# Joining two tiled matmul steps of a chunked linear attention, under a list scheduler's due times

## The chip, the cores and the metric

The kernel runs on one core of a Trainium2 chip. The metric is the device time of one execution in microseconds (us). The median of three runs is compared; a separate execution was recorded by the hardware profiler.

## The reference, cut to what matters

The input `x` is (8, 1024, 256) in fp32: 8 sequences of 1024 rows. Four blocks follow each other, each as `x = x + block(layernorm(x))`:

```
# 1: flow ("linear") attention with 16 heads of width 16, then its own FFN (256 -> 1024 -> 256, gelu)
q = sigmoid(heads(Wq));  k = sigmoid(heads(Wk));  v = heads(Wv)
# sink_in, src_out, cons_sink, cons_src: cumulative sums over the rows of q and k, per head
vs = v * src_comp
kv = cumsum(einsum('bhld,bhlm->bhldm', k, vs), axis=2)        # causal state
x  = einsum('bhld,bhldm->bhlm', q * sink_in/normal, kv) * sink_alloc
h  = layernorm(inputs + x @ Wo + bo);   out = layernorm(h + gelu(h @ W1 + b1) @ W2 + b2)
# 2: dense FFN 256 -> 1024 -> 256 with relu
# 3: full softmax attention over 1024 rows, one head of width 256
# 4: gated FFN 256 -> 704 -> 256, activations and weights rounded block by block to FP4
```

The change lies in block 1. There the causal state is computed chunk by chunk: for a chunk of 128 rows, the output is the masked product `(q k^T) vs` inside the chunk plus `q` times the state `kv` of all chunks before it; then the chunk's own `k^T vs` is added to the state.

## The kernel before, in words

**Tiling.** Rows are handled in chunks of 128 and in groups of four chunks (512 rows). There are 16 groups, two to a sequence; `p` is the group, `i` the chunk in it (0 to 3), `c = 4p + i` the chunk's number. A group goes through block 1 and 2 in about 147 us, and the softmax and FP4 blocks of sequences that are finished run beside the later groups' linear attention and dense blocks, until about 2420 us.

**Engines.** TensorE (PE in the profile) does all products. It is used in two ways: full 128x128 products, and *tiled* ones, in which the array is cut into four tiles, 32x128 for the scores of four heads side by side, and 128x32 for products whose output is 32 wide. All is fp32: each matmul leaves two records in the profile, a transpose one.

**One chunk of linear attention** (`linear_chunk`, line 1284) has two tiled steps on PE:

- the *scores* (lines 1367 to 1385): 16 matmuls `kz` x `q` of tile size 32x128 into four PSUM banks. VectorE multiplies each bank with the causal mask `tri` into a tile `sc` of the pool `flow`;
- the *values* (lines 1406 to 1458): 8 matmuls `q` x `kv_sum` (the state so far), 16 matmuls `sc` x `v_pad`, both accumulating in one bank, and, but for a sequence's last chunk, 8 matmuls `k` x `vs` for the state. All have tile size 128x32. ScalarE copies the result to `xo`, VectorE masks the state's increment, GpSimd adds it to `kv_sum`, and a full product with `wo` follows.

Full products of the dense blocks (`half` x `w_in`, then `hidden` x `w_out`), of the softmax block (`n2T,wqk` makes `qT`; `n2T,qT` the scores; `vt,probT` the values) and of the FP4 block (`xqT` with `wgT` and `wuT`, `hqT` with `wdT`) fill the time between.

**Order.** The kernel is written as generators that yield what they need. `Plan.run` (line 375) is a list scheduler that runs while the program is built: of all parts it takes the one with the smallest key

```
key = wait, unripe, queue == "tensor", not stays, part[2]
```

`wait` comes from a model of each engine's durations in `Plan.took`; `stays` prefers a tiled step right behind a tiled step, with 0.3 us of leniency in `wait`; `part[2]` is the due time, `at`. Due times are sums of constants from the table `T`, and from `EARLY`, which gives other constants while the planned time lies under 130, 260, 400 and 2150 us and from there on. The order of issue on every engine is fixed by this.

**Transposes** (`flip`, line 734) go one of two ways. If the planner finds a product ready within `ahead` us, GpSimd copies the tile (`cut`), a transposing DMA issued by SP turns it (`spun<-cut`), and ScalarE copies it to its place. If it finds none (`plan.idle`), two PE transposes (`bank<-ident,...`) are used instead, and ScalarE copies from PSUM.

**Dense blocks.** `half` is a pair of transposed chunks; eight steps of `half` x `w_in`, bias and gelu or relu on ScalarE (`hidden`), and `w_out` make one half of a group. `behind` lets two `hidden` tiles be outstanding, and is emptied when the next `half` isn't ready.

Of the kernel before, what the change touches and what calls it, by code (L numbers as in the profile page):

```python
# [17 lines left out]
P = 128  # L18
# [7 lines left out]
HB = P // 2  # L26
SCW = P + HB
# [4 lines left out]
    span=-0.073, prods=0.129, pair=0.137, sums=0.037, weighted=0.239, sums2=0.231, chunk=0.625,  # L32
    scores=0.819, turn_k=0.829, xo=0.419, turn_h=0.635, step=0.092, dense=-0.115, norm=0.522,
    soft=3.5, soft1=0.277, soft2=0.575, soft3=0.75, fp4=2.397, fp4_over=4.836, tail=11,
    weights=0.209, shy=0.745, ripe_t=1.247, ripe_v=0.744, ripe_s=0.298, ripe_g=0.0, ripe_d=6.94,
    back=0.511, ahead=0.946, stage=3, lin=0.0, lin0=0.01, lin1=0.0, lin2=0.0, lin3=0.0,
    dense0=0.0, dense1=-0.033, norm0=0.0, norm1=0.0, weights0=-0.412, weights1=0.023, gate0=0,
    gate1=1, by_act=1,
)
LAG = 2  # L40
QB = 16
G = 4
GT = G * P
# [18 lines left out]
    "norm": (3, D, F32),  # L62
    "hidden": (LAG + 2, D, F32),
    "soft": (5, D, F32),
# [15 lines left out]
        prods=0.359, pair=0.052, weighted=0.011, sums2=0.405, scores=0.861, turn_k=0.81,  # L80
        xo=0.296, step=0.131, dense=0.051, soft=2.551, soft1=0.323, soft2=0.706, fp4_over=5.754,
        weights=0.044, ripe_t=1.058, ripe_v=0.456, ripe_s=0.249, ripe_g=0.541, ripe_d=9.276,
        lin3=0.344, dense1=-0.003, weights0=-1.017, weights1=0.043,
    )),
    (260.0, dict(
        span=-0.064, prods=0.185, sums=-0.114, chunk=0.702, scores=0.785, dense=-0.085,
# [4 lines left out]
        prods=-0.044, turn_k=0.82, turn_h=0.707, step=0.103, norm=0.746, soft=3.784, soft3=0.912,  # L91
        fp4=2.195, weights=0.078, ripe_d=7.2, ahead=0.839, lin2=-0.414,
    )),
    (2150.0, dict(
        prods=0.106, pair=0.211, sums=0.071, weighted=0.176, chunk=0.596, turn_k=0.801, xo=0.47,
        turn_h=0.706, soft3=1.013, fp4=3.733, fp4_over=6.383, weights=0.169, ripe_d=6.945,
        ahead=0.541, lin1=0.497, lin2=-0.186, lin3=-0.528, dense0=-0.017, dense1=0.151,
        norm0=-0.113, weights0=-0.286, gate1=3,
    )),
    (1000000000.0, dict(  # L100
        lin3=0.54, ripe_d=5.647, lin1=0.423, dense1=-0.052, scores=0.713, xo=0.287, chunk=0.609,
        shy=0.81, back=0.523, sums2=0.353,
    )),
]

# [18 lines left out]
class Plan:  # L124
# [203 lines left out]
    def pe(self, *tiles, **kw):  # L328
        return self.need("tensor", tiles, **kw)

    def dve(self, *tiles, **kw):
        return self.need("vector", tiles, **kw)
# [108 lines left out]
def block_stack_kernel(ctx: ExitStack, tc: tile.TileContext, a: dict, out: bass.AP):  # L441
# [20 lines left out]
    plan = Plan(tc, tc.nc)  # L462
# [5 lines left out]
    nc, pe, dve, act, dma = plan, plan.pe, plan.dve, plan.act, plan.dma  # L468
    x_dram = a["L0_attn_inputs"]
    B, L, _ = x_dram.shape  # L470
# [13 lines left out]
    def mm_bank():  # L484
        bank = ps.tile([P, 512], F32, tag="bank", name="bank")
        plan.bank(bank)
        return bank
# [25 lines left out]
    def small(shape, name, bufs=4):  # L513
        t = sm.tile(shape, F32, tag=name, name=name, bufs=bufs)
        return t
# [77 lines left out]
    later = make("q_c", "later")[:, : GT + P]  # L593
# [197 lines left out]
    def blocks(t, width):  # L791
        return t[:, :width].rearrange("p (b e) -> p b e", e=QB)

    def wide(v, rows, nb):
        return v.unsqueeze(2).to_broadcast([rows, nb, QB])

    def fp4(src, width, rows=P, factor=1.0):
# [7 lines left out]

        nb = width // QB
        src = src[:rows, :width]
        amax = small([P, INTER // QB], "x_amax", 2)[:rows, :nb]
        nc.vector.tensor_reduce(
            amax, blocks(src, width), AX.X, ALU.max, apply_absolute_value=True  # L810
        )
        sc = small([P, INTER // QB], "x_s", 4)[:rows, :nb]
        nc.vector.tensor_scalar(sc, amax, factor / 6.0, 1e-12, ALU.mult, ALU.max)
        rc = small([P, INTER // QB], "x_r", 3)[:rows, :nb]
        nc.vector.reciprocal(rc, sc)
# [118 lines left out]
    weights = set()  # L934
# [59 lines left out]
    def running(out, cur, carry, b, first, last):  # L994
# [14 lines left out]
    flows = B * NG  # L1009
    seqs = [{"past": {"chunks": 0}, "n2T": {}, "vt": {}, "normed": 0} for _ in range(B)]  # L1010
    groups = [
        {"res": {}, "hT": {}, "nT": {}, "turned": {}, "scaled": set(), "ran": set()}
        for _ in range(flows)
    ]
    count = {
# [268 lines left out]
    def linear_chunk(p, i, n0T, comp, qk):  # L1284
# [7 lines left out]
            banks=1,  # L1292
            when=lambda: count["v"] == c and c - count["attended"] < V_PADS and "v" in late,
        )
        bank = mm_bank()
        for k in range(2):
            nc.tensor.matmul(
                bank[:, :D],
                lhsT=n0T[:, k, here],
                rhs=wqkv[2][:, k, :],  # L1300
                start=k == 0,
                stop=k == 1,
# [27 lines left out]
        for e in range(2):  # L1330
            into_pad(nc.scalar.copy, e, 1 - e)

        by_act = p < T["by_act"]
        tile_kz = yield from fresh(
            "flow",
            act(
                qk[1],
                at=at + times["scores"] + times["step"] * i,
                when=lambda: (
                    c - count["scored"] < 2 if by_act  # L1340
                    else i in groups[p]["scaled"] and count["scored"] == c
                )
# [6 lines left out]
        kz = tile_kz.rearrange("p (k b e t) -> p k b e t", k=2, b=2, e=2)  # L1349
# [6 lines left out]
            )  # L1356
        kz = tile_kz.rearrange("p (k b n) -> p k b n", k=2, b=2)

        if by_act:
            yield pe(  # L1360
                tile_kz, qk[0], later, banks=4,
                when=lambda: i in groups[p]["scaled"] and count["scored"] == c,
            )
            count["scored"] += 1
        else:
            yield pe(tile_kz, qk[0], banks=4, tiled=True)
        banks = [mm_bank()[:, : 2 * SCW] for _ in range(4)]
        for bank in banks:
            if by_act:
                nc.tensor.matmul(  # L1370
                    bank, lhsT=later[:, GT:], rhs=later[:, : 2 * SCW], start=True, stop=False,
                    skip_group_check=True,
                )
        for k in range(2):
            for b in range(2):
                for r, bank in enumerate(banks):
                    rows = slice(32 * r, 32 * r + 32)
                    nc.tensor.matmul(
                        bank[:, k * SCW + b * P : k * SCW + P + b * HB],
                        lhsT=kz[rows, k, b, :],  # L1380
                        rhs=qk[0][rows, k, i * P + b * HB : (i + 1) * P],
                        start=not by_act,
                        stop=True,
                        skip_group_check=True,
                    )
        plan.drop(tile_kz)
        scores = []
        for bank in banks:
            sc = yield from fresh("flow", (act if by_act else dve)(bank), "sc")
            sc = sc[:, : 2 * SCW].rearrange("p (k n) -> p k n", k=2)  # L1390
            bank = bank.rearrange("p (k n) -> p k n", k=2)
# [8 lines left out]
        if not end:  # L1400
# [2 lines left out]
            kT = two((yield from fresh("lin", need, "k")))  # L1403
            yield from flip(qk[1][:, :, here], kT, near=p == 0)
        kv = past.get("kv")
        yield pe(
            pad,
            vs,
            *scores,
            *([] if kv is None else [kv]),  # L1410
            *([] if end else [kT]),
            banks=1,
            tiled=True,
            when=lambda: count["attended"] == c,
        )
# [5 lines left out]
        bank = both[:, :D]  # L1421
        for k in range(2):
            for r in range(4):
                if kv is not None:
                    nc.tensor.matmul(
                        bank[32 * r : 32 * r + 32, k * P : (k + 1) * P],
                        lhsT=kv[:, k, 32 * r : 32 * r + 32],
                        rhs=qk[0][:, k, here],
                        start=k == 0,
                        stop=False,  # L1430
                        skip_group_check=True,
                    )
        for k in range(2):
            for b in range(2):
                for r in range(4):
                    nc.tensor.matmul(
                        bank[32 * r : 32 * r + 32, k * P + b * HB : (k + 1) * P],
                        lhsT=pad[:, b, 4 * k + r, :],
                        rhs=scores[r][:, k, b * P : P + b * HB],
                        start=kv is None and k == 0 and b == 0,  # L1440
                        stop=k == 1 and b == 1,
                        skip_group_check=True,
                    )
        plan.drop(*scores)
        if not end:

            kvbank = both[:, D : D + 64].rearrange("p (k d) -> p k d", k=2)
            for k in range(2):
                for r in range(4):
                    nc.tensor.matmul(  # L1450
                        kvbank[32 * r : 32 * r + 32, k, :],
                        lhsT=kT[:, k, 32 * r : 32 * r + 32],
                        rhs=pair_columns(vs, 4 * k + r),
                        start=False,
                        stop=True,
                        skip_group_check=True,
                    )
            plan.drop(kT)
        plan.drop(vs)
        xo = two((yield from fresh("lin", act(bank), "xo")))  # L1460
        nc.scalar.copy(xo, two(bank))
# [24 lines left out]
        bank = mm_bank()  # L1486
        for k in range(2):
# [14 lines left out]
            when=lambda: half_fits(p, "hT", i // 2) and count["dense"] >= p - 1,  # L1502
# [16 lines left out]
    def dense():  # L1519
# [44 lines left out]
        def load_weights(names, used, loaded, first):  # L1564
# [3 lines left out]
            for p in range(flows):  # L1568
                for name in names:
                    for f in 2 * list(range(0, NF, 2)):  # L1570
                        yield dma(
                            at=p + 0.9 + due("weights", p) + (2 * n % 32 + (0 if first else LAG)) / 32,
                            when=lambda: n < bufs + used[0] // 2 and count["stage"] >= 2,
# [20 lines left out]
        for p in range(flows):  # L1594
            for b, (kind, ba, func) in enumerate((("hT", b1, AF.Gelu), ("nT", fb1, AF.Relu))):
                for half in range(2):
# [3 lines left out]
                    for f in range(NF):  # L1600
# [22 lines left out]
                        if f == NF - 1:  # L1623
                            count["halves"] -= 1
                        if len(behind) > LAG:
                            yield from second()
# [271 lines left out]
```

## Time and profile before

| | |
|---|---|
| median of 3 runs | 2450.55 us (2448.66 to 2452.24) |
| the profiled execution's own time | 2450.4 us |
| its span, first to last instruction | 2448.7 us |
| PE (matmuls) busy | 2419.4 us, 99% |
| VectorE (DVE) busy | 1914.3 us, 78% |
| ScalarE (ACT) busy | 1387.7 us, 57% |
| GpSimd (POOL) busy | 1276.9 us, 52% |
| transposing DMAs `spun<-cut` | 768 |

The page gives busy time by engine, then the span in 40 slices, the chain of work that ended last, and groups of instructions with the mean duration of one. The end of a matmul is modelled and overlaps its successor, so that starts are more exact than durations: back to back, two records of a 256-column matmul start 0.216 us apart. In the timeline, equal instructions that follow each other are one row: start, busy time, name, count of records, and in brackets the engine's idle time before the row and what ended it.

### The profile page before, as it was taken

Reading aid. Unit: us, or ns where it says so; the run is one execution under the profiler, and the core shown is the slowest. Engines: PE = TensorE matmul, PEld = TensorE weight load, DVE = VectorE, ACT = ScalarE, POOL = GpSimd, SP = SyncE. Lnnn points to the kernel's source line nnn. Section 1 sums busy time; section 2 is a strip of 40 time slices with the busy share of each in tenths; the row PEclk is TensorE's granted clock in tenths of the full one; section 3 lists DMA queues with packets and bytes.
Section 4 is the critical chain, followed back from the end, with each engine's and each line's share of the span. In section 5 each row is a group of like instructions: output and inputs, shape, how many; then the busy total and the mean of one; then the engine's idle time right before and its main releaser. Section 6 shows DMA issues by size and latency. Waiting matters only on the chain.

```text
span 2448.7 us, 47669 instructions
## 1 busy us (share of the span) xinstructions
PE 2419.4 (99%) x16473; PEld 1891.6 (77%) x16473; DVE 1914.3 (78%) x4152; ACT 1387.7 (57%) x2895; POOL 1276.9 (52%) x2258
## 2 busy tenths in 40 slices
PE   8999999999999999999999999999999999999999
PEld 6877777777877777777777777777777777887777
DVE  7778787878779787787877888688886978765887
ACT  5454556565565645656565565655556465555454
POOL 4354556565555656365563655546555474544342
PEclk9999999999999999999999999999999999999999
DMA  3355455564655555546555554556545555545332
GB/s 106 91 150 160 123 151 128 139 146 121 145 135 121 140 139 129 138 115 155 132 122 134 125 150 125 139 131 124 141 127 133 143 118 145 124 126 129 67 83 59
DMA packets 630897, 312.74 MB, mean 128 GB/s; under 512 B 434304, under 2 KB 619136, under 8 KB 630656
## 3 DMA queue, kind: packets, MB, share of 16 engines
q1 hardware_dynamic: 630656, 309.70, 51.3%
q8 instruction: 130, 2.13, 0.4%
q14 instruction: 111, 0.91, 0.1%
HBM read 188.17 MB, written 20.71 MB: 85 GB/s over the span
## 4 chain that ended last, share of the span: by engine, by line
PE 88%; DVE 6%; DMA 2%; POOL 2%; issue 1%; ACT 1%; SPq 0%; DVEq 0%; POOLq 0%; ACTq 0%
PE bank L422 88%; DMA spun<-cut 2%; DVE hid L422 1%; POOL cut L422 1%; DVE prod L422 1%; DVE ln_st L422 1%; DVE n L422 0%; POOL ln_rstd L422 0%; DVE sc L422 0%; DVE mx L422 0%; DVE res L422 0%; DVE u L422 0%; SPq L422 0%; POOL ln_shift L422 0%; DMA w_in<-in_L_attn_W_dram 0%
## 5 line engine op out<-in xcount | busy, mean ns | idle before, releaser
L422 PE MATMUL bank<-half,w_in 128*128 128x256 f32 x2048 | 529.2, 381 | 9.5 <-ACT half L422 6.4
L422 PE MATMUL bank<-w_out,hidden 128*128 128x256 f32 x2048 | 525.6, 383 | 1.5 <-DMA w_out<-in_L_attn_W_dram 1.4
L422 PEld LDWEIGHTS bank<-w_out,hidden 128*128 128x128 f32 x2048 | 377.4, 190 | 105.1 <-issue 45.7
L422 PEld LDWEIGHTS bank<-half,w_in 128*128 128x128 f32 x2048 | 384.5, 190 | 87.9 <-issue 22.4
L422 POOL TENSOR_SCALAR ln_ve<-ln_mv 128x1 f32<-128x1 f32 x384 | 107.1, 279 | 510.6 <-DVE ln_mv L422 489.4
L422 POOL TENSOR_TENSOR ln_rstd<-ln_ve,neghalf 128x1 f32<-128x1 f32 x384 | 251.3, 654 | 32.0
L422 ACT ACTIVATE hidden<-bank,c_L_ffn_b 128x256 f32<-128x256 f32 x256 | 120.8, 472 | 223.8 <-PE bank L422 222.0
L422 PE MATMUL bank<-n2T,qT 128*128 128x512 f32 x512 | 241.5, 594 | 0.0
L422 PE MATMUL bank<-vt,probT 128*128 128x256 f32 x1024 | 231.2, 379 | 0.0
L422 PEld LDWEIGHTS bank<-vt,probT 128*128 128x128 f32 x1024 | 194.2, 190 | 32.9 <-issue 6.9
L422 POOL COPY cut<-n 128x512 uint16<-128x512 uint16 x233 | 175.0, 757 | 79.8 <-DVE n L422 68.4
L422 ACT ACTIVATE hidden<-bank,c_L_attn_b 128x256 f32<-128x256 f32 x256 | 119.7, 469 | 170.8 <-PE bank L422 170.0
L422 POOL COPY cut<-prob 128x512 uint16<-128x512 uint16 x213 | 147.8, 716 | 92.0 <-ACT prob L422 50.4
L422 POOL COPY cut<-hid 128x512 uint16<-128x512 uint16 x172 | 116.4, 694 | 144.3 <-DVE rsum L422 66.3
L422 PE MATMUL bank<-wdT,hqT 128*128 128x256 f32 x768 | 175.9, 379 | 0.0
L422 PE MATMUL bank<-wgT,xqT 128*128 128x352 f32 x512 | 173.8, 462 | 0.5 <-ACT xqT L422 0.5
L422 PE MATMUL bank<-wuT,xqT 128*128 128x352 f32 x512 | 172.3, 459 | 0.0
L422 ACT COPY probT<-spun 128x512 uint16<-128x512 uint16 x250 | 159.6, 674 | 13.3 <-DMA spun<-cut 12.8
L422 PEld LDWEIGHTS bank<-wdT,hqT 128*128 128x128 f32 x768 | 145.6, 190 | 22.7 <-issue 1.9
L422 ACT ACT_TABLE_LOAD x124 | 159.1, 1283 | 4.4 <-PE bank L422 2.2
L422 PEld LDWEIGHTS bank<-n2T,qT 128*128 128x128 f32 x512 | 96.4, 190 | 69.7 <-issue 56.4
L422 PEld LDWEIGHTS bank<-wuT,xqT 128*128 128x128 f32 x512 | 97.3, 190 | 54.2
(272 smaller groups left out, 4831.1 us busy)
## 6 DMA issues: line engine op xcount, KB each, us to landing
w_in<-in_L_attn_W_dram SPq DMA_DIRECT2D x128, 256.0 KB
w_out<-in_L_attn_W_dram SPq DMA_DIRECT2D x128, 256.0 KB
w_in<-in_L_ffn_w_dram SPq DMA_DIRECT2D x128, 256.0 KB
w_out<-in_L_ffn_w_dram SPq DMA_DIRECT2D x128, 256.0 KB
spread<-packed SPq DMA_DIRECT2D x90, 256.0 KB
spun<-cut SPq DMA_TRANSPOSE x768
x<-in_L_attn_inputs_dram SPq DMA_DIRECT2D x64, 128.0 KB
xr<-in_L_attn_inputs_dram SPq DMA_DIRECT2D x64, 128.0 KB
```

The costliest lines, as they stand in the source:

```text
L422: ins = method(*args, **kw)
```

## The change

The scores of chunk `i` (`i` > 0) in groups 4 to 15 are no longer a PE step of their own. The chunk prepares `kz`, leaves its `score` function in `groups[p]["asked"]`, and waits until its banks exist. The values step of chunk `i - 1` waits until the next chunk has asked, demands five free PSUM banks instead of one and the next chunk's `kz` and `q`, and issues the 16 score matmuls directly behind its own. So 36 chunks of 64 are joined this way; groups 0 to 3 and each group's chunk 0 stay as they were.

```diff
+JOIN = 4
...
+        joined = p >= JOIN and i > 0
+        if joined:
+            asked = groups[p]["asked"][i] = SimpleNamespace(tile=tile_kz, run=None, banks=None)
+        elif by_act:
...
+        def score():
+            banks = [mm_bank()[:, : 2 * SCW] for _ in range(4)]
...
+            plan.drop(tile_kz)
+            return banks
+
+        if joined:
+            asked.run = score
+            yield dve(when=lambda: asked.banks is not None)
+            banks = asked.banks
+        else:
+            banks = score()
...
+        joins = p >= JOIN and i < G - 1
+        nexts = groups[p]["asked"]
+        if joins:
+            yield dve(when=lambda: i + 1 in nexts)
         yield pe(
             pad,
             vs,
             *scores,
             *([] if kv is None else [kv]),
             *([] if end else [kT]),
-            banks=1,
+            *([nexts[i + 1].tile, qk[0]] if joins else []),
+            banks=5 if joins else 1,
             tiled=True,
             when=lambda: count["attended"] == c,
         )
...
+        if joins:
+            nexts[i + 1].banks = nexts[i + 1].run()
```

The constants of the two last stretches of `EARLY` (planned time 400 to 2150 us, and from 2150 us on) are replaced by other ones, about half of them changed and some added, among them `norm` (0.522 to 0.652), `sums2` (0.231 to 0.365), `turn_h` (0.706 to 0.798) and `span` (-0.073 to 0.034) in the first, `scores` (0.713 to 0.599), `soft3` (0.75 to 1.132) and `fp4` in the second. Constants of single early groups (`lin1`, `dense0`, `norm0` and the like) are among them too, though those groups lie before 400 us.

More of the change, by code (lines that the diff above doesn't have):

```diff
@@ L94 @@
     (2150.0, dict(
[L95 to L98, printed above, removed]
+        span=0.034, prods=0.067, pair=0.211, sums=0.071, weighted=0.176, sums2=0.365,
+        chunk=0.596, turn_k=0.822, xo=0.47, turn_h=0.798, step=0.05, dense=-0.126, norm=0.652,
+        soft3=1.013, fp4=3.733, weights=0.169, ripe_s=0.404, ripe_d=6.945, ahead=0.541,
+        lin1=-0.157, lin2=-0.457, lin3=-0.528, dense0=-0.29, weights0=-0.071, weights1=0.189,
+        gate1=3, dense1=-0.093, norm0=0.859,
     )),
     (1000000000.0, dict(
-        lin3=0.54, ripe_d=5.647, lin1=0.423, dense1=-0.052, scores=0.713, xo=0.287, chunk=0.609,
-        shy=0.81, back=0.523, sums2=0.353,
+        lin3=0.291, ripe_d=5.647, lin1=0.423, dense1=-0.096, scores=0.599, xo=0.287, gate0=2,
+        chunk=0.609, back=0.523, sums2=0.353, span=-0.107, step=0.03, ripe_s=0.0, ripe_v=1.131,
+        pair=0.076, turn_k=0.932, lin=-0.077, weights1=-0.123, soft3=1.132, fp4=0.958,
+        dense=-0.015, prods=0.27, sums=0.215, weights=0.124,
     )),
@@ L1011, in block_stack_kernel @@
     groups = [
-        {"res": {}, "hT": {}, "nT": {}, "turned": {}, "scaled": set(), "ran": set()}
+        {"res": {}, "hT": {}, "nT": {}, "turned": {}, "scaled": set(), "ran": set(), "asked": {}}
         for _ in range(flows)
@@ L1357, in linear_chunk @@
         kz = tile_kz.rearrange("p (k b n) -> p k b n", k=2, b=2)
-        if by_act:
+        joined = p >= JOIN and i > 0
+        if joined:
+            asked = groups[p]["asked"][i] = SimpleNamespace(tile=tile_kz, run=None, banks=None)
+        elif by_act:
             yield pe(
@@ L1366, in linear_chunk @@
             yield pe(tile_kz, qk[0], banks=4, tiled=True)
[L1367 to L1377, printed above, removed]
-                    nc.tensor.matmul(
[L1379 to L1383, printed above, removed]
+        def score():
+            banks = [mm_bank()[:, : 2 * SCW] for _ in range(4)]
+            for bank in banks:
+                if by_act:
+                    nc.tensor.matmul(
+                        bank, lhsT=later[:, GT:], rhs=later[:, : 2 * SCW], start=True, stop=False,
                         skip_group_check=True,
                     )
-        plan.drop(tile_kz)
+            for k in range(2):
+                for b in range(2):
+                    for r, bank in enumerate(banks):
+                        rows = slice(32 * r, 32 * r + 32)
+                        nc.tensor.matmul(
+                            bank[:, k * SCW + b * P : k * SCW + P + b * HB],
+                            lhsT=kz[rows, k, b, :],
+                            rhs=qk[0][rows, k, i * P + b * HB : (i + 1) * P],
+                            start=not by_act,
+                            stop=True,
+                            skip_group_check=True,
+                        )
+            plan.drop(tile_kz)
[6 more added lines that the diff above has]
+            banks = score()
         scores = []
```

## Prediction

> **What bounds the kernel now.** I read the page first, for the engine that never rests and for the clock.
>
> ```profile
> span 2448.7 us, 47669 instructions
> ...
> PE 2419.4 (99%) x16473; PEld 1891.6 (77%) x16473; DVE 1914.3 (78%) x4152; ACT 1387.7 (57%) x2895; POOL 1276.9 (52%) x2258
> ...
> PEclk9999999999999999999999999999999999999999
> ```
>
> PE is busy 99% at full clock, and matmuls are 88% of the chain of waits. The orders of before and after are the same until some 450 us, so the stretches after 400 us count; the table by windows and PE's own waits for 400 to 2150 us say how full they are.
>
> ```profile
> 1000.00:2150.00 1150.00, 1146.85 (x7846) 897.07 (x7845) 916.85 (x1957) 664.82 (x1360) 629.85 (x1098) 1.00 0.54 133
> 2150.00:2420.00 270.00, 269.54 (x1159) 202.34 (x1158) 195.36 (x440) 145.98 (x300) 107.23 (x199) 1.00 0.42 97
> ```
>
> ```profile
> PE bank L422 <- ACT half L422: 4.8, 6, 0.9
> ```
>
> Columns: stretch, length, then busy time of PE, weight loads, DVE, ACT, POOL. PE stands still 4.8 us in 1750, six times, always for `half`. Hence nothing but PE's own work and those waits can be won here, and every transpose or mode change that PE does more or less is paid or won in full.
>
> **The change part by part.**
>
> *Joined steps.* The timeline of PE shows a values step alone, a scores step alone, and one where the planner had already put them together:
>
> ```profile
> 1084.39 1.03 PE L422 MATMUL bank<-half,w_in 128*128 128x256 f32 x4
> ...
> 1086.70 1.13 PE L422 MATMUL bank<-half,w_in 128*128 128x256 f32 x4
> 1087.67 1.24 PE L422 MATMUL bank<-wdT,hqT 128*128 128x256 f32 x5
> ...
> 1097.20 1.88 PE L422 MATMUL bank<-n2T,qT 128*128 128x512 f32 x4
> ...
> 1100.06 1.13 PE L422 MATMUL bank<-wv,n2T 128*128 128x256 f32 x4
> 1101.03 1.03 PE L422 MATMUL bank<-w_out,hidden 128*128 128x256 f32 x4
> ...
> 1110.51 1.03 PE L422 MATMUL bank<-half,w_in 128*128 128x256 f32 x4
> ...
> 1113.88 1.13 PE L422 MATMUL bank<-w_out,hidden 128*128 128x256 f32 x4
> 1114.85 1.03 PE L422 MATMUL bank<-half,w_in 128*128 128x256 f32 x4
> ```
>
> From the start of the full row in front to the start of the second row behind, less the full records between (0.216 us each for 256 columns, 0.429 for 512): values 3.28 - 8 x 0.216 = 1.55; scores 3.83 - 4 x 0.429 - 4 x 0.216 = 1.25; both together 4.34 - 8 x 0.216 = 2.61. Joining saves 0.20 us (0.198 unrounded). The 21 such steps of before are equal within 3 ns. In the instruction order of the changed kernel 36 scores follow values directly instead of 21, and the crossings between full and tiled products fall from 295 to 265: **15 x 0.198 = -3.0 us**.
>
> A rule speaks against more. The Trainium skill, TensorEngine Tiling (Array Packing), Key Properties: changing the tiling mode drains the array. Scores are 32x128 and values 128x32, so a joined step still has one change inside: of four drains one is saved. TensorE: Matmul & The Clock Gate, Single matmul latency, puts a drain at some 175 ns; 15 x 0.175 would be -2.6 us, an estimate. I take the row. The same tiling page, PSUM Bottleneck, says that PSUM evacuation may become the limit: five banks are asked for at once, and DVE's `sc` takes 0.544 us a bank. If each of the 15 new joins waited for one, that would be +8.2 us. The row says nothing is lost: the 21 joined steps show no idle time in front or inside. I take 0 and keep +8.2 as upper end.
>
> *Transposes.* The new due times let the planner find PE about to run dry more often: 19 more pairs of transposes (prob 11, n 6, hid 5, k 1, h 4 fewer) go to PE, and `spun<-cut` falls from 768 to 749. A pair's price:
>
> ```profile
> 1077.14 0.38 PE L422 MATMUL bank<-ident,k 128*128 128x128 f32 x2
> 1077.36 1.35 PE L422 MATMUL bank<-wgT,xqT 128*128 128x352 f32 x4
> ...
> 1080.51 0.31 PE L422 MATMUL bank<-vs,k 128*32 128x32 f32 x16
> 1081.69 1.13 PE L422 MATMUL bank<-half,w_in 128*128 128x256 f32 x4 [0.88 <-ACT half L422]
> ```
>
> 0.22 us from start to start: **19 x 0.22 = +4.2 us**. What they leave is off the path: 19 `cut` on POOL (0.72 us each), 19 DMAs on SP's queue, and 19 ACT copies get shorter. ACT receives 19 layernorm applications from DVE (0.60 us each) and 6 table loads (1.28 us each); at 57% busy it hides 19 us, unless they stand in front of a copy PE waits for, which is the first rival.
>
> *Waits that go.* The last row above is the wait for `half`: `vs,k` to `half` takes 1.18 us from start to start, against 0.23 behind the next values step (1086.47 to 1086.70). The time is once in each 294 us, five times, 0.86 on average, and 1.1 us at 596 us. In the new order `half` is completed by a PE transpose at this place, so I let all six go, **-5.4 us**, and also the 0.5 us at 2417 us, where `xqT` is now transposed earlier: **-0.5 us**.
>
> *Waits that come.* In each period from some 900 us on the new order has a thin place: `n2T,wqk`, directly `n2T,qT`, a pair `ident,n`, a pair `ident,prob`, `half,w_in`. Here `qT` has no cover at all. Before, a scores step stands between:
>
> ```profile
> 1064.51 1.05 PE L422 MATMUL bank<-n2T,wqk 128*128 128x128 f32 x8
> ...
> 1066.54 1.98 PE L422 MATMUL bank<-n2T,qT 128*128 128x512 f32 x4
> ```
>
> ```profile
> 1065.60 0.62 ACT L422 ACTIVATE qT<-bank,bqk 128x128 f32<-128x128 f32 x2 [1.12 <-PE bank L422]
> ```
>
> The last `wqk` record starts at 1064.51 + 7 x 0.112 = 1065.29, `qT` is done at 1066.22: with 0.05 for the semaphore the products can start 0.98 us after it. Uncovered they would start after 0.11: 0.87 us of wait, **5 x 0.87 = +4.4 us**. Then `half`: a PE transpose at 2417.5 us is followed by its waiting product 0.735 us later (ACT's copy in between takes 0.37); the pair `ident,prob` covers 0.33 of it: **5 x 0.41 = +2.0 us**. At some 2320 us one more `qT` is covered by one pair only: **+0.7 us**. At the place that waits today, `half` is copied by ACT behind `hid`, about 0.2 us late: **5 x 0.2 = +1.0 us** (0 to 0.5 each).
>
> *The rest.* Scores of a chunk 0 now stand 5.7 us of PE work ahead of their values, not 10; DVE needs at most 5.4. A values step that waits for the next `kz` holds `xo`, `kv_sum` and the next `wo` behind it; `kz` had at least 1.5 us to spare everywhere. The four `sc` tiles live longer; late next would be `prod`, with 2.6 us to spare. The tail behind the last `wuT` (24 us) keeps 24 full `wdT`, and DVE's work in it is 13.3 us instead of 13.6 by the durations of the rows: 0, with 1 us either way.
>
> Sum: -3.0 + 4.2 - 5.4 - 0.5 + 4.4 + 2.0 + 0.7 + 1.0 = +3.4 us. The profiled execution took 2450.4 us, as the median (2450.55) to 0.01%; so **2453.8 us**.
>
> **The rivals.**
>
> *Queues are late at the thin places (slower).* At both places of each period PE has nothing else to do, so lateness of ACT is paid 1:1. There ACT's order is: `half` copied from a transposing DMA, `ahead`, both `qT`, layernorm `n`, `half` from PSUM. If that DMA lands late, all behind it is late. For it: today's wait is of this kind, a DMA of 2.55 us in front of `half`. Against it: three other `half` classes have 2 us to spare. From 0.3 us of extra delay per period the sum passes +4.9 us, 0.2%; with today's 0.86 in each of 5 periods it gives 2458, in both places 2462.
>
> *The thin places are covered (faster).* If the first `qT` product waits only for the first of the two activations, some 0.3 us each goes (1.5 in all); if the two pairs of transposes there lie in time in which PE would have waited anyway, 0.44 each (2.2), and the waits for `half` vanish (3.0): -6.7, 2447.1. If besides a join saved two drains of the cited 0.175 us instead of 0.198, another -2.3: 2444.8. Against it: transposes stand in PE's queue in order and delay what follows, and the joined rows are exact.
>
> *The joins don't bite.* Five banks at once hold PE, or hold softmax steps back: up to +8.2, 2462. The 21 joined steps speak against it.
>
> **How the numbers follow.** A measurement of this kernel tells about 0.2%, 4.9 us, from no change. Forecast as priced, within that: 0.50. Late queues: 0.34, of which nearly all beyond +4.9. Joins that wait: 0.06, slower. Covered: 0.10, of which I count all as faster, though its first part alone stays just within. Faster 0.10, within 0.50, slower 0.40. The range takes the forecast with its bounds and most of the late queues: 2447 to 2463; the forecast's own is 2450 to 2455.5.
>
> **What would show it.** Right: 36 joined steps of 2.61 us each and 30 fewer crossings; idle PE in front of `n2T,qT` (0.8 to 0.9) and `half,w_in` (0.4), once each in 294 us; 749 transposing DMAs. Wrong: idle time in front of a joined step; waits of PE in 400 to 2150 us under 3 us or over 12 us in all; a tail longer than 25.5 us.

## The result, and the profile after

The changed kernel takes 2455.24 us (median of 12 runs, 2452.86 to 2458.17), the kernel before 2451.61 us (12 runs beside them, 2448.63 to 2453.41): a ratio of 1.0017, 95% interval 1.0009 to 1.0025. That is 3.6 us more: a small slowdown that is clear of the scatter, and inside the 4.9 us (0.2%) within which the prediction's most likely case lay. The prediction said 2453.8, and +3.4 us.

The profiled execution took 2452.86 us with a span of 2451.0. First the page after, which answers to the lines of the page before:

```profile
span 2451.0 us, 47543 instructions
...
PE 2422.4 (99%) x16509; PEld 1894.2 (77%) x16509; DVE 1902.4 (78%) x4133; ACT 1394.3 (57%) x2923; POOL 1260.0 (51%) x2239
...
PEclk9999999999999999999999999999999999999999
...
PE 93%; DVE 3%; DMA 1%; ACT 1%; POOL 1%; issue 0%; SPq 0%; DVEq 0%; ACTq 0%; POOLq 0%
...
spun<-cut SPq DMA_TRANSPOSE x749
```

PE has 36 records more: 38 transposes, less one filler product (two records). The 749 transposing DMAs are the 19 fewer that were counted from the order. PE remains the bound, with 93% of the chain. The windows and PE's waits for 400 to 2150 us (total, times, longest) come next:

```profile
1000.00:2150.00 1150.00, 1147.19 (x7769) 896.03 (x7768) 908.68 (x1926) 676.68 (x1389) 614.79 (x1075) 1.00 0.54 131
2150.00:2420.00 270.00, 268.75 (x1240) 202.13 (x1239) 190.67 (x439) 145.41 (x296) 114.47 (x207) 1.00 0.45 100
```

```profile
PE bank L426 <- ACT qT L426: 2.3, 5, 0.5
PE bank L426 <- ACT half L426: 1.2, 5, 0.2
PE bank L426 <- ACT hidden L426: 1.0, 1, 1.0
PE bank L426 <- ACT n0T L426: 0.2, 1, 0.2
```

The five `half` waits of 0.9 us are gone. In their place stand five for `qT` and five others for `half`, the ones that the prediction named, and two that it did not name. In the 1150 us window PE is busy for 1147.2 us, where it was 1146.9 before: the waits were exchanged.

Here is a joined step on PE's timeline, one that the kernel before had as two steps:

```profile
1100.70 1.03 PE L426 MATMUL bank<-half,w_in 128*128 128x256 f32 x4
1101.66 0.64 PE L426 MATMUL bank<-q,kv_sum 128*32 128x128 f32 x16
1102.12 0.84 PE L426 MATMUL bank<-sc,v_pad 128*32 128x128 f32 x32
1102.78 0.31 PE L426 MATMUL bank<-vs,k 128*32 128x32 f32 x16
1103.02 1.12 PE L426 MATMUL bank<-q,kz 32*128 32x128 f32 x32
1104.07 1.13 PE L426 MATMUL bank<-w_out,hidden 128*128 128x256 f32 x4
1105.03 1.03 PE L426 MATMUL bank<-wv,n0T 128*128 128x256 f32 x4
```

No row has a bracket, so nothing is waited for. From 1100.70 to 1105.03, less 8 x 0.216, is 2.60 us, the price that the prediction read from the joined steps of before (2.61).

And here is the thin place of each period, PE first, then ScalarE:

```profile
1194.36 1.14 PE L426 MATMUL bank<-n2T,wqk 128*128 128x128 f32 x8
1195.95 1.98 PE L426 MATMUL bank<-n2T,qT 128*128 128x512 f32 x4 [0.46 <-ACT qT L426]
1197.77 0.38 PE L426 MATMUL bank<-ident,n 128*128 128x128 f32 x2
1197.99 0.38 PE L426 MATMUL bank<-ident,prob 128*128 128x128 f32 x2
1198.62 1.13 PE L426 MATMUL bank<-half,w_in 128*128 128x256 f32 x4 [0.24 <-ACT half L426]
1199.59 0.27 PE L426 MATMUL bank<-ident,scale 128*128 128x128 f32 x1
```

```profile
1195.53 0.63 ACT L426 ACTIVATE qT<-bank,bqk 128x128 f32<-128x128 f32 x2 [0.84 <-PE bank L426]
```

The bracket (0.46 and 0.24) is shorter than the loss, because the modelled end of a matmul reaches into the gap. Counted from start to start, less the usual pitch of the row in front (its time from one start to the next when nothing is waited for), the waits are 0.62 and 0.41 us.

The same count over all PE records, from one and the same instruction (at 456.6 us before, 454.9 after) to the last one, shows where the time went. Each record's start-to-start time is split into the pitch of its kind and what lies over it:

| part of PE's time | before, us | after, us | difference |
|---|---|---|---|
| tiled steps and their crossings | 154.8 | 151.8 | -3.0 |
| transposes on PE | 6.5 | 10.7 | +4.2 |
| filler products | 6.6 | 6.1 | -0.5 |
| waits | 12.1 | 15.3 | +3.2 |

That is +3.9 of the +4.1 us between those two instructions; full products make the small rest. In front of them the orders are equal, and the after trace happens to be 1.7 us faster there, which is why the spans differ by 2.3 only. Of the eleven traces seven reach this instruction at 456.5 to 456.8 us, two at 458.5 to 458.6 and one at 460.6, though all have the same PE order up to it. So traces are best compared from here on.

### The profile page after: what moved, and what is told of

The parts are those of the page before. It is cut to its first block, busy times and chain, and to the rows that moved or that the text cites. A ratio compares the mean times of both kernels' runs of the same rounds, so it can differ in the third digit from the quotient of the medians.

```text
span 2451.0 us, 47543 instructions
## 1 busy us (share of the span) xinstructions
PE 2422.4 (99%) x16509; PEld 1894.2 (77%) x16509; DVE 1902.4 (78%) x4133; ACT 1394.3 (57%) x2923; POOL 1260.0 (51%) x2239
## 4 chain that ended last, share of the span: by engine, by line
PE 93%; DVE 3%; DMA 1%; ACT 1%; POOL 1%; issue 0%; SPq 0%; DVEq 0%; ACTq 0%; POOLq 0%
PE bank L426 93%; DMA spun<-cut 1%; DVE prod L426 1%; SPq L426 0%; DVE hid L426 0%; DVE k L426 0%; DMA w_in<-in_L_attn_W_dram 0%; POOL ln_rstd L426 0%; DMA b_L_attn_bo<-in_L_attn_bo_dram 0%; POOL ln_shift L426 0%; DVE u L426 0%; DVE ln_st L426 0%; DVE q L426 0%; ACT L426 0%; DVE x_amax L426 0%
## 5 line engine op out<-in xcount | busy, mean ns | idle before, releaser
L426 POOL TENSOR_SCALAR ln_ve<-ln_mv 128x1 f32<-128x1 f32 x384 | 117.0, 305 | 603.0 <-DVE ln_mv L426 588.3
L426 POOL TENSOR_TENSOR ln_rstd<-ln_ve,neghalf 128x1 f32<-128x1 f32 x384 | 244.4, 637 | 31.9
L426 POOL COPY cut<-n 128x512 uint16<-128x512 uint16 x227 | 161.7, 719 | 115.7 <-DVE n L426 84.8
L426 POOL COPY cut<-prob 128x512 uint16<-128x512 uint16 x214 | 152.8, 737 | 81.4 <-ACT prob L426 42.4
L426 POOL COPY cut<-hid 128x512 uint16<-128x512 uint16 x167 | 127.7, 782 | 82.6 <-DVE hid L426 43.8
L426 ACT COPY probT<-spun 128x512 uint16<-128x512 uint16 x239 | 154.3, 671 | 11.1 <-DMA spun<-cut 10.9
```

The source lines that it names most:

```text
L426: ins = method(*args, **kw)
```

## The experiments

Each was timed beside the kernel before on one chip; ratios are to it. "Us more than the changed kernel" is worked out from differences to the kernel before, +3.6 for the change.

**1. The joins with the old due times.** Both changed stretches of `EARLY` get their old constants; `JOIN` stays at 4.

```diff
-         span=0.034, prods=0.067, pair=0.211, sums=0.071, weighted=0.176, sums2=0.365,
...
+         prods=0.106, pair=0.211, sums=0.071, weighted=0.176, chunk=0.596, turn_k=0.801, xo=0.47,
...
-         chunk=0.609, back=0.523, sums2=0.353, span=-0.107, step=0.03, ripe_s=0.0, ripe_v=1.131,
...
+         lin3=0.54, ripe_d=5.647, lin1=0.423, dense1=-0.052, scores=0.713, xo=0.287, chunk=0.609,
```

> The joined steps with the due times of before. Theory (PE is full, so the time is PE's own work plus its waits): by the order of its instructions it has the same 265 crossings as the changed kernel (-3.0 us against before), but 207 transposes of tiles on PE where before has 157 and the changed kernel 195 (+5.5 us), and five products of qT without cover (0.6 us each), so 3 to 10 us slower than before: 2454 to 2462. Rival (the new due times are what costs, the joins alone are a gain): about 3 us faster than before, 2448.6.

Measured: 2483.71 us against 2449.93, ratio 1.0133 (1.0117 to 1.0148). Both theories missed it by over 20 us.

**2. The new due times without the joins.**

```diff
-JOIN = 4
+JOIN = 16
```

> The new due times without any joined step. Theory: its order has 327 crossings where before has 295 (+3.2 us), 12 more transposes on PE (+1.3 us), and waits of 0 to 5 us more: 2455 to 2461. Rival (the new due times are better by themselves and the joins cost): at or below before, 2451.6 or less.

Measured: 2478.88 us against 2449.93, ratio 1.0113 (1.0099 to 1.0127). Missed as well. PE's waits from 450 us on, of experiment 1 first, then of experiment 2 (the longest groups of each):

```profile
PE bank L423 <- ACT half L423: 5.3, 7, 1.3
PE bank L423 <- ACT hidden L423: 3.8, 5, 1.5
PE bank L423 <- ACT xqT L423: 3.4, 5, 1.1
```

```profile
PE bank L426 <- POOL kv_sum L426: 3.8, 3, 2.0
PE bank L426 <- ACT xqT L426: 3.8, 4, 1.7
PE bank L426 <- ACT half L426: 3.8, 3, 2.9
```

The waits no longer repeat at one place of each period; they are scattered over all inputs of PE. By the count from start to start:

| us, difference to the kernel before | joins alone | due times alone |
|---|---|---|
| tiled steps and crossings | -3.0 | +3.2 |
| transposes on PE | +5.5 | +1.3 |
| filler products | +5.6 | +3.5 |
| waits | +25.0 | +21.8 |

The joins alone save exactly the same 3.0 us of crossings, and the other order loses 36 us on the rest. So here the two halves of the change cannot be priced apart: each without the other gives a worse order, 34 and 29 us slower than the kernel before, and the sum of the prediction holds only because it was made from the one order that was run. Why these two orders are so much worse, no run took apart. (Filler products are `ident` products that the planner inserts where it foresees PE idle for over 1.6 us: 163 and 155 of them instead of 141, in part a loss that it saw itself.)

**3. and 4. A full product inside the joined steps, and in front of them.** In each of the 36 joined steps an extra 128x128 product of `ident` is issued, between values and scores (3) or in front of the values (4). Everything else keeps its place.

```diff
+def quiet(bank_):
+    took, plan.took = plan.took, lambda *args: None
+    nc.tensor.matmul(bank_, lhsT=ident, rhs=ident, start=True, stop=True)
+    plan.took = took
...
+if joined:                     # 3, in score()
+    quiet(banks[0][:, :P])
...
+if joins:                      # 4, in front of the values
+    quiet(both[:, :P])
```

> The changed kernel with one more full 128x128x128 product (two records of 0.112 us) between the values and the scores in each of the 36 joined steps; order and everything else are the same. Theory: each costs 0.224 of work and one more crossing of 0.198, so 36 x 0.422 = +15.2 us against the changed kernel. Rival (a joined step saves nothing, because 128x32 to 32x128 is a change of mode as well): 36 x 0.224 = +8.1 us.

> The control: the same 36 products, in front of the values instead, where PE is in full mode anyway. Both theories: 36 x 0.224 = +8.1 us against the changed kernel; the difference to the one with the product in between is 7.1 us if a crossing costs 0.198 us[...], and 0 by the rival.

Measured: 2469.11 us (ratio 1.0075, 1.0062 to 1.0088) and 2463.52 us (1.0049, 1.0036 to 1.0062), the spans 2467.4 and 2461.0. One and the same step, first of 3, then of 4:

```profile
1107.45 1.03 PE L426 MATMUL bank<-half,w_in 128*128 128x256 f32 x4
...
1109.53 0.31 PE L426 MATMUL bank<-vs,k 128*32 128x32 f32 x16
1109.76 0.49 PE L426 MATMUL bank<-ident 128*128 128x128 f32 x2
1110.18 1.12 PE L426 MATMUL bank<-q,kz 32*128 32x128 f32 x32
...
1112.20 1.03 PE L426 MATMUL bank<-wv,n0T 128*128 128x256 f32 x4
```

```profile
1105.52 1.03 PE L426 MATMUL bank<-half,w_in 128*128 128x256 f32 x4
1106.39 0.38 PE L426 MATMUL bank<-ident 128*128 128x128 f32 x2
...
1107.82 0.31 PE L426 MATMUL bank<-vs,k 128*32 128x32 f32 x16
1108.06 1.12 PE L426 MATMUL bank<-q,kz 32*128 32x128 f32 x32
...
1110.08 1.03 PE L426 MATMUL bank<-wv,n0T 128*128 128x256 f32 x4
```

From the start of the first to the start of the last of these rows are 4.75 and 4.56 us, with the same work between, so the product inside costs 0.19 more (0.198 unrounded) than the one in front.

The control is 13.6 - 3.6 = 10.0 us above the changed kernel by the medians, and 10.0 by the spans. In the traces 1.7 us of the 10.0 lie ahead of the first join, where the two kernels are equal; from there on it is 8.2, of which the products themselves are 36 x 0.224 = 8.1. The kernel with the product inside pays 5.6 us more than the control by the medians, 6.4 by the spans. Tiled steps and crossings differ by 7.1 us in the count, 36 x 0.198, and one wait at 535 us that is 0.5 us shorter gives some back. So a pair of crossings costs 0.198 us in either place, and the join is worth what the prediction took.

**5. The transposes twice.** Each of the 98 PE transposes that the planner inserts after 450 us is issued twice.

```diff
+            if plan.free.get("tensor", 0.0) > 450.0:
+                took, plan.took = plan.took, lambda *args: None
+                for k in range(2):
+                    nc.tensor.transpose(bank[:, k, :], src[:, k, :], ident)
+                plan.took = took
```

> The changed kernel, in which every transpose of a tile on PE from some 450 us on is issued twice (98 more transposes, same result, same order otherwise). Theory (PE is full, a transpose is paid 1:1 at 0.109 us unless it fills a wait): 10.7 us, less 1.3 for the 12 in the waits of the tail and less 1.3 where the second pair of the thin place, or the pair ahead of the uncovered qT at 2320 us, covers a wait: +8 us against the changed kernel. Rival (the transposes stand where PE would wait anyway, so they are nearly free): +3 us or less.

Measured: 2466.06 us against 2452.0, ratio 1.0058 (1.0043 to 1.0073): some 10 us more than the changed kernel. The count gives +10.3 us in all, and +10.7 for the 98 transposes, 0.109 each. PE's waits after 450 us:

```profile
PE bank L426 <- ACT qT L426: 2.6, 6, 0.5
PE bank L426 <- DVE k L426: 0.9, 1, 0.9
PE bank L426 <- ACT hqT L426: 0.9, 1, 0.9
PE bank L426 <- ACT xo L426: 0.6, 2, 0.3
```

`half` has left the list: its wait falls from 0.41 to 0.19 us, because the pair in front is longer. Other waits come, for `xo` and `hqT`, so that all in all only 0.4 us of waits go, where 2.6 had been expected. Transposes on PE are paid for nearly 1:1, which speaks against the part of the "covered" rival that let them lie in waiting time.

**6. `qT` later.** ScalarE writes the first half of `qT` twice, so that `qT` is complete one activation later.

```diff
+        took, plan.took = plan.took, lambda *args: None
+        nc.scalar.activation(qT[:, 0, :], bank[:, :P], AF.Identity, bias=bqk[:, 0:1])
+        plan.took = took
```

> The changed kernel, in which ScalarE does the first of the two activations of each qT twice (64 more activations of 0.36 us, some 0.27 us each back to back; same order). Theory (only uncovered qT is paid): the wait of PE for qT grows from 0.62 to some 0.9 us at five thin places and at 2320 us, +1.6 us in all, nothing elsewhere. Rival (ScalarE's queue is as tight as PE's, so that lateness spreads to half, hidden and xo): +5 us or more, with new waits of PE for half, hidden and xo.

Measured: 2458.84 us against 2452.0, ratio 1.0029 (1.0017 to 1.0041), about 3 us more than the changed kernel. The waits:

```profile
PE bank L426 <- ACT qT L426: 5.4, 6, 1.1
...
PE bank L426 <- ACT half L426: 1.2, 5, 0.2
```

The same six waits for `qT`, each 0.40 us longer (0.62 to 1.02 at the thin place, 0.90 to 1.30 at 2320 us), and no seventh: the `qT` of all other score steps has cover enough. By the count the wait for `xo` at 694 us grows from 0.20 to 0.57, and 0.49 for `xqT` at 2426 us is new. The rival had expected 5 us or more; these two are all that shows of it. The theory held, with an activation that costs 0.40, not the 0.27 that I had taken. The three activations take 1.03 us in this trace instead of 0.63 for two, so the step is what the row shows.

**7. New constants for the first stretch only.** The stretch from 2150 us on gets its old constants.

```diff
-         lin3=0.291, ripe_d=5.647, lin1=0.423, dense1=-0.096, scores=0.599, xo=0.287, gate0=2,
...
+         lin3=0.54, ripe_d=5.647, lin1=0.423, dense1=-0.052, scores=0.713, xo=0.287, chunk=0.609,
```

> Joined steps, new due times for the stretch 400 to 2150 us, the old ones from 2150 us on. Theory (the loss of the joins under the old constants sits in the long stretch): 12 more transposes and 4 more fill products than the changed kernel in its order and two more uncovered qT, +1 to +6 us against the changed kernel, 2456 to 2461, and the same waits as the changed kernel up to 2150 us. Rival (the last stretch is where the constants matter): 2465 or more.

Measured: 2460.12 us against 2452.0, ratio 1.0033 (1.002 to 1.0045). Until 2150 us its waits are those of the changed kernel, but for one at 538 us that is 0.3 us longer. So, with the joins in place, nearly all of the 30 us that experiment 1 lost hang on the constants of the 400 to 2150 us stretch; those of the last stretch are worth 4 to 5.

**8. and 9. Two banks at the thin place.** In 8 the two halves of `wqk`'s product go into two PSUM banks, so that PE can signal the first half when it is done, and the first `qT` activation needn't wait for the second. In 9, in addition, the two transposes of a `half` go into two banks with two copies. The order of issue stays, but for each of those copies being two.

```diff
-        bank = mm_bank()
+        bank = mm_bank()
+        second = ps.tile([P, 512], F32, tag="bank", name="bank")
+        parts = [bank[:, :P], second[:, :P]]
...
-                    bank[:, e * P : (e + 1) * P],
+                nc.tensor.matmul(parts[e], **kw)
...
-                qT[:, e, :], bank[:, e * P : (e + 1) * P], AF.Identity, bias=bqk[:, e : e + 1]
+            nc.scalar.activation(qT[:, e, :], parts[e], AF.Identity, bias=bqk[:, e : e + 1])
...
+                nc.scalar.copy(dst[:, 0, :], bank[:, 0, :])      # 9
+                nc.scalar.copy(dst[:, 1, :], second[:, :P])      # 9
```

> The changed kernel with the two halves of wqk's product in two PSUM banks instead of one, so that the first qT activation can start when its own 4 records are done instead of all 8; order of issue on every engine as in the changed kernel. Theory (the qT wait is the time from the last wqk record to the first activation's result, and the activation waits for the bank, not for its own half): the 4 records are 0.44 us, so each wait falls from 0.62 to about 0.18, 5 times, and the one at 2320 us by 0.4: 2.6 us less than the changed kernel, about 2452.6; the half waits stay at 0.41. Rival (the activation is held by ScalarE or by semaphores whatever it reads, or one more bank in the rotation holds PE elsewhere): no gain, 2455 or more, qT waits of 0.5 and over.

> As e8_qT_two_banks, and where PE transposes a half (from group 4 on) its two transposes go into two banks and are copied by two ScalarE copies of 128 columns, the first of which can start one transpose earlier. Theory (the first product with half waits only for its own 128 rows): 0.11 us for the transpose and some 0.1 us for the shorter copy, so the wait falls from 0.41 to about 0.2, 5 times: 1.0 us less than e8, about 2451.6, as fast as the kernel before. Rival (the product waits for the whole tile half, and the second copy only adds a fixed cost): half waits of 0.5 or more, 2453 or more.

Measured: 2455.63 us (ratio 1.0012, 1.0003 to 1.002) and 2454.89 us (1.001, 1.0002 to 1.0019) against 2452.5. By time neither can be told from the changed kernel: the savings of 2.6 and 3.6 us that had been expected are not there. The traces show the step itself, and where its gain went. The thin place in experiment 8, PE and ScalarE:

```profile
1198.51 1.14 PE L426 MATMUL bank<-n2T,wqk 128*128 128x128 f32 x8
1199.66 1.98 PE L426 MATMUL bank<-n2T,qT 128*128 128x512 f32 x4
```

```profile
1199.24 0.81 ACT L426 ACTIVATE qT<-bank,bqk 128x128 f32<-128x128 f32 x2 [0.40 <-PE bank L426]
```

From the `wqk` row to the `qT` row it is now 1.15 us instead of 1.59: the wait went from 0.62 to 0.17, as expected, five times. The wait at 2320 us, which was to fall by 0.4 too, stayed at 0.89: there ScalarE is still busy with `hqT` when the products are done, so that an earlier signal gains nothing. In experiment 9 PE's waits for 400 to 2150 us read:

```profile
PE bank L426 <- ACT hidden L426: 1.2, 1, 1.2
PE bank L426 <- DVE scale L426: 1.0, 5, 0.2
```

`qT` and `half` are both off the list (0.17 and 0.19 us by the count), and VectorE's `scale` is on it, five times. The transpose of `scale` is the next row behind `half,w_in`. It had no slack left, and waits 0.16 us in experiment 8 and 0.37 in 9. So of the 2.25 + 1.1 us taken away in 9, 1.85 come back one row later. The wait for `hidden` at 532 us varies between traces that have the same order around it (1.19 after, 2.01 in 8, 1.36 in 9, 0.87 in 3), and that hides the rest: from the end of the common order on, both traces are only 0.4 us shorter than that of the changed kernel. Neither version beats the kernel before.

## Why the prediction was right, point by point

- *Joined steps, -3.0.* Right: -2.96 us in the count, 36 joined steps, none with idle time in front or inside, and experiments 3 and 4 gave 0.198 us by a second way. That five banks are asked for at once cost nothing, so the rival of joins that don't bite is out.
- *Transposes, +4.2.* Right to 0.1 us, and experiment 5 shows that they are paid for in full.
- *Waits that go, -5.9.* Right for those it listed: the five waits for `half` (4.26 us by the count), 1.08 us at 596 us and 0.63 at 2417 us, together 5.97. It missed one: the row of `q,kz` at 507 us took 2.02 us to the next full product instead of 1.05, and these 0.97 us went too; what held it is not known.
- *`qT` at the thin place, +4.4.* Right place, right number of waits, and the size too high: 5 x 0.62 = 3.1, and 0.10 more on the pitch of each following product, which the prediction did not have. The failed term is the ready time of `qT`. I let the first product wait for both activations, 0.98 us behind the last `wqk` record. It waits for the first only and starts 0.73 behind (at 1195.95 in the rows above, while the two activations last until 1196.16). That was the first half of the "covered" rival, about as large as it said. Experiments 6 and 8 move this wait up and down by what they add and take away.
- *`half` at the thin place, +2.0.* Right: 5 x 0.41 = 2.05.
- *`qT` at 2320 us, +0.7.* 0.90 measured, and the size is luck. With the ready time that the other five show and one pair as cover it would have been 0.62 - 0.22 = 0.40. ScalarE was late here, with `hqT` copies in front of `qT` and no idle time:

```profile
2319.36 1.25 ACT L426 COPY hqT<-spun 128x512 uint16<-128x512 uint16 x2
2320.51 0.63 ACT L426 ACTIVATE qT<-bank,bqk 128x128 f32<-128x128 f32 x2
```

- *The place that waited before, +1.0.* Too high: it has no wait. In the trace `half` is copied at 1076.96, right behind `hid` as forecast, and is complete at 1077.63; its first product starts at 1077.80. The copy that completes this `half` is that of a transposing DMA; the PE transpose by which the prediction let this wait go makes the other chunk of the pair (copied at 1073.69). So the wait went, with 0.17 us to spare, but not for the reason given.
- *Not forecast:* 1.19 us for `hidden` at 532 us, 0.33 for `n0T` at 544, 0.84 for `flow` at 2392, 0.2 for `xo` at 692. The first has a table load in front of an activation that PE waits for, which the prediction had put at nothing as long as it does not stand there. ScalarE's timeline around it:

```profile
530.90 0.67 ACT L426 COPY probT<-spun 128x512 uint16<-128x512 uint16 x1 [0.39 <-DMA spun<-cut]
531.59 1.28 ACT L426 ACT_TABLE_LOAD   x1
532.88 0.20 ACT L426 ACTIVATE table<-one 128x1 f32<-128x1 f32 x1
532.99 0.82 ACT L426 ACTIVATE hidden<-bank,c_L_attn_b 128x256 f32<-128x256 f32 x2
```

  From the start of that `probT` copy, which waits for its transposing DMA, PE's product follows 2.60 us later in all eight traces with this order, and half of that is the table load. What varies between traces of one and the same PE order is when the DMA lands: in experiment 8 the copy starts 0.8 us later behind its `cut` than in the changed kernel, and the wait is 2.01 us instead of 1.19.

- *The tail, 0.* Right: from the last `wuT` on 23.8 us before and 23.5 after.

The overall +3.4 against +3.6 is partly luck. The `qT` term and the place that waited before were too high by 2.3 us, and 1.5 us (the wait at 507 us, the fewer filler products) went uncounted; the unforeseen waits (2.6) and the longer pitches behind ten waits (1.0) took about as much back. "Late queues", the strongest rival, did not come where it was looked for: the waits at the thin place repeat to 0.01 us in all five periods, and in experiments 3, 4 and 7 too. At two other places lateness does reach PE: of a DMA at 532 us, which the prediction had not named, and of ScalarE at 2320.

## What to carry to other kernels

On a saturated engine whose order is fixed when the program is built, count records, crossings and transposes from the two orders, price each by its start-to-start time, and then walk through the places where the new order has no cover; that gave the size of the result to a few us (that it came within 0.2 us was luck). The diff alone could not have: the same joins under the old constants cost 34 us. Don't price the halves of such a change apart: joins without the new due times, or due times without the joins, cost some 30 us, most of it in scattered waits. The old constants went with the old list of steps, the new with the new. When a wait is shortened at a thin place, look at the next input in line first (here `scale`), for here it gave back more than half.

## What the runs showed of the hardware

- The last full record in front of a tiled step takes 0.093 us longer from start to start (0.309 instead of 0.216 for 256 columns), the first one behind it 0.104 longer (0.320): together the 0.198 of experiments 3 and 4. A joined step saves just this pair. The change of tile shape inside it (128x32 to 32x128) is not free: from the last `vs,k` record to the next are 0.125 us, to a score in the changed kernel as to the full product in experiment 3, while `vs,k` records in a row stand 0.007 to 0.012 apart. From the first tiled record to the next full one a joined step takes 2.408 us, exactly the 1.358 of values and the 1.050 of scores that stand alone.
- After a wait of PE the next full product's pitch is 0.104 us longer too (behind all ten of the `qT` and `half` waits, and still behind the 0.17 us that are left in experiment 8), so that a wait of 0.41 costs 0.5. A transpose pays 0.056 in either place, behind a tiled step or a wait.
- That the first `qT` activation waited for both halves is the program's doing: in the trace of the changed kernel PE updates the semaphore once, behind the last of the eight `wqk` records; in experiment 8 it does so behind the fourth and the eighth, and the activation starts 0.44 us earlier, four records of 0.112.
- The scatter between runs goes in part with the granted clock: of 25 runs of the kernel before beside experiments 8 and 9, the spans average 2449.2 us at a mean clock of 0.999 (6 runs), 2450.4 at 0.998 (9) and 2452.4 at 0.997 (9). It is not the clock alone: beside experiments 5 to 7, on another chip, 6 runs at 0.997 average 2450.7. In the profiled executions of before and after the first 100 us run at 0.97, and in experiment 8 the stretch from 200 to 300 us at 0.98. At 0.999 the changed kernel's span averages 2452.7 (6 runs), and that of the kernel before 2448.3 to 2449.2 on three other sets of runs: 3.4 to 4.4 us more, which agrees with the medians.
